# Storing rows and their factors from one tile, loading two experts' weights together, and joining statistics before the squares, in a two-layer attention and mixture-of-experts kernel

## The chip, the cores and the metric

The kernel runs on 1 core of one Trainium2 chip. The metric is the device time of one execution in microseconds (us), as the median of several runs; smaller is better.

## The reference

The input x has 8 batches of 256 tokens of 256 features (2048 tokens, fp32), and a context of the same size. Two layers follow, each an attention and a feed-forward part with residuals.

```python
x = x + _L0_xattn_ref(_layernorm(x), ctx, ctx, Wq, bq, Wout, bout)
x = x + _L0_ffn_ref(_layernorm(x), centroids, ln_g, ln_b, w1, b1, w2, b2)
x = x + _L1_xattn_ref(_layernorm(x), ctx, Wq, bq, Wkv, bkv, Wp, bp)
x = x + _L1_ffn_ref(_layernorm(x), gate_W, w1_e, w3_e, w2_e, w1_s, w3_s, w2_s)
```

- The attention of layer 0 is an autocorrelation: FFT products averaged over everything, the top 12 lags with softmax weights, a weighted sum of rolled values, and an output projection. Its result is added to x.
- The feed-forward of layer 0 assigns tokens to 8 experts in balance: expert e, in turn, takes the 256 tokens with the highest score (normalised row times its centroid) among those not yet taken. Each expert computes `routed + gelu(layer_norm(routed) @ w1 + b1) @ w2 + b2`, and the rows go back to their tokens.
- Layer 1 is a cross attention with 16 heads over the context, and a mixture of 8 experts (two for each token, 256 by 1024) beside 8 shared ones. It is the larger part of the time and the change does not touch it.

## The kernel before

**Staging.** Everything runs in one program. Its tokens lie as 16 tiles of 128 rows: `X` is [128, 16, 256], two tiles to a batch. Each engine runs its instructions in the order in which the program was written, and SP does the same with the DMAs that it issues; a DMA uses one of eight semaphores in turn, and waits for the DMA eight before it on the same one. So the order of the statements sets the order of the work, on each engine and in SP's queue. PE gets its spare work from a list of small steps (`work`): `fill` takes as many steps as should fill the time between two rounds of a search. Those are key and value projections of layer 1, and later the experts' products.

**The rows after attention, by batch (lines 1833 to 2003).** PE copies X's rows into PSUM by an identity matmul (`copy_rows`, 1833), adds the attention's row PB through a `spread` matrix (`spread_rows`, 1844), and the result goes back to X by an ACT copy. `column_norms` (1370, called at 1885) computes bounds for a later quantity: four small matmuls, an ACT scaling and two POOL operations. `small_products` (1866) are other small matmuls.

For the first three batches `take` (1990) computes raw `bn_stats` on DVE; for the fourth, ACT computes sums with the copy (`act_sums`, 2007) and then squares (2026); for the others DVE computes statistics whole (`tile_stats`). `put_together` (1971) turns six raw statistics into variances with six small POOL operations, `factors` (2039) calls `rstd` (1457), which starts with a POOL power (1465) and ends in `newton`, four small operations (1468 to 1471) for the reciprocal standard deviation. The factors (that and minus mean times it) lie in `rm`, [128, 16, 2]. `widen` (2043) spreads them to 32 columns, `factor_rows` (1950) turns them into rows of PSUM (`psr`), `factors_out` (2061) copies these to `srow`, and `times_factors` (2058) multiplies the raw scores with them. The two halves of expert 0's scores become `n`, those of all experts `SC`; SC's second half is made on POOL (2122).

**Through memory.** `SC` is stored to `SCd` (2173), from which `load_row` (2161) loads each expert's 2048 scores: a source of four outer steps (groups of 512 scores), each repeated to 32 partitions. The rows of X are stored to `NMd` in DRAM (2048 rows of 258), as each batch is done (2000 and 2017), and their factors into the last two columns by four stores of 8-byte pieces (`store_factors`, 1936). `Yd` (2177) is blanked, 2 MB, as is the end of `Od` (2181).

**The search (2184) and the list (2242).** For each expert, five rounds: DVE counts scores above a threshold (2198), PE sums the counts (`pcn`, 2215), DVE finds the next threshold. `list_tokens` makes the indices `ids` of the taken tokens with small matmuls, and POOL gathers their rows with factors from NMd into R (2323), in two gathers of 128 rows. Expert e's list is made while expert e+1 is searched. Then `ffn` (2358) is called: ACT normalises R (2367), PE transposes it (`turn_rows`, 2387), ACT writes RT (2391), PE multiplies with w1 (`ph`, 2404), and so on to the addition of b2b on DVE and the scatter to Yd (2431).

**Weights.** `load_l0` (1812) loads w1 and w2 of one expert, 1 MB each, into a pool of two buffers (w0). Those of expert 0 are loaded at 1822, those of expert 1 after the last `take`. Later ones follow as buffers come free.

The order around the change, as written:

```python
take(b[6:])
W0[1] = load_l0(1)
newton_3, means_3 = factors(12, 16, nc.vector)
newton_a(nc.vector)
widen(0, 8, nc.scalar)
...
nc.sync.dma_start(out=SCd, in_=SC)
for m in range(2):
    store_factors(m)
rows = {e: load_row(e) for e in range(1, 3)}
```

Of the kernel before, what the change touches and what calls it, by code (L numbers as in the profile page):

```python
# [9 lines left out]
F32 = mybir.dt.float32  # L10
# [9 lines left out]
P = 128  # L20
# [1066 lines left out]
def fast_path(  # L1087
# [33 lines left out]
    nc = tc.nc  # L1121
    B, S, D = x.shape
    T = B * S
    NT = T // P
    KC = D // P
    TPB = S // P
# [7 lines left out]
    NB = D // P  # L1134
# [12 lines left out]
    res = ctx.enter_context(tc.tile_pool(name="res", bufs=1))  # L1147
    small = ctx.enter_context(tc.tile_pool(name="small", bufs=3))
    dram = ctx.enter_context(tc.tile_pool(name="dram", bufs=1, space=DRAM))
    X = res.tile([P, NT, D], F32, name="X")  # L1150
    hn = ctx.enter_context(tc.tile_pool(name="hn", bufs=2))
    nfine = res.tile([P, 1], F32, name="nfine")
    bad0 = res.tile([P, 1], F32, name="bad0")
# [143 lines left out]
    for dst, src, i in (  # L1297
# [12 lines left out]
        out=WZ[:, :, DH : 2 * DH],  # L1310
# [59 lines left out]
    def column_norms(pn):  # L1370

        for c in range(NB):
            for kc in range(KC):
                nc.tensor.matmul(
                    pn[:, c : c + 1],
                    wsq[:, kc, c * P : (c + 1) * P],
                    ones[:, 0:1],
                    start=(kc == 0),
                    stop=(kc == KC - 1),
                )  # L1380
        nc.scalar.activation(qmax, pn, AF.Copy, scale=257.0)
        nc.gpsimd.tensor_tensor(
            qmax, qmax, powers[:, 1:2].to_broadcast([P, NB]), ALU.pow
        )
        nc.gpsimd.tensor_tensor(qmax, qmax, babs, ALU.add)
# [426 lines left out]
    def load_l0(e):  # L1812
        w1 = w0.tile([P, KC, F], F32, tag="w1", name=f"w1_{e}")
        nc.sync.dma_start(out=w1, in_=L0_ffn_w1[e].rearrange("(kc p) f -> p kc f", p=P))
        w2 = w0.tile([P, NF, D], F32, tag="w2", name=f"w2_{e}")
        nc.sync.dma_start(out=w2, in_=L0_ffn_w2[e].rearrange("(fc p) d -> p fc d", p=P))
        return w1, w2

    NMd = dram.tile([T, D + 2], F32, name="NMd")
    Yd = dram.tile([T, D], F32, name="Yd")  # L1820
    Td = dram.tile([E * CAP1 + P, ROW], F32, name="Td")
    Od = dram.tile([T + P, D], F32, name="Od")
    W0 = {0: load_l0(0)}


    order_b = [2 * g + m for m in range(2) for g in range(4)]
# [1 line left out]
    pos = {}  # L1828

    def rows_of(b):  # L1830
        return X[:, TPB * b : TPB * (b + 1), :]

    def copy_rows(b, pool, tag):
        pos[b] = pool.tile([P, TPB, D], F32, tag=tag, name="po")
        nc.tensor.matmul(
            pos[b].rearrange("p h d -> p (h d)"),
            ident,
            rows_of(b).rearrange("p h d -> p (h d)"),
            start=True,
            stop=False,  # L1840
            skip_group_check=True,
        )
# [23 lines left out]
    def small_products(j):  # L1866
        for dc in range(KC):
            nc.tensor.matmul(
                pw[:, j, :],
                wrt[:, dc, j * P : (j + 1) * P]  # L1870
                if j < 2
                else boc[:, dc : dc + 1].to_broadcast([P, P]),
                cenP[:, dc, :],
                start=(dc == 0),
                stop=(dc == KC - 1),
            )
# [2 lines left out]
    copy_rows(order_b[1], ps_t, "pt")  # L1879
    small_products(0)  # L1880
    small_products(1)
    copy_rows(order_b[2], ps_t, "pt")
    small_products(2)
    nc.tensor.matmul(pb, ones[:E, :], bdiag, start=True, stop=True)
    column_norms(pw[:, 4, 0:NB])
    nc.vector.tensor_copy(WCn, pw[:, 0:3, :])
    bound = pr.tile([P, E], F32, name="bound")
    nc.vector.tensor_copy(bound, pb)
# [44 lines left out]
    rowv = NMd.rearrange("(c p) d -> p c d", p=P)  # L1933
    sexp = pa.tile([P, NT, 32], F32, name="sexp")

    def store_factors(m):
        for h in range(TPB):
            nc.sync.dma_start(
                out=NMd.rearrange("(g m h p) d -> m h p g d", m=2, h=TPB, p=P)[m, h][
                    :, :, D:  # L1940
                ],
                in_=rm[:, 8 * m : 8 * m + 8, :].rearrange(
                    "p (g h) d -> h p g d", h=TPB
                )[h],
            )


    psrs = []
# [22 lines left out]
    def put_together(q1):  # L1971

        d, v = (
            small.tile([P, q1], F32, tag=f"pt_{x_}", name=f"pt_{x_}") for x_ in "dv"
        )
        m = MV[:, 0:q1, 0]
        nc.gpsimd.tensor_tensor(d, st6[:, :, 1], st6[:, :, 4], ALU.subtract)
        nc.gpsimd.tensor_tensor(v, st6[:, :, 2], st6[:, :, 5], ALU.add)
        nc.gpsimd.tensor_tensor(d, d, d, ALU.mult)
        nc.gpsimd.tensor_scalar(d, d, D / 4.0, None, ALU.mult)  # L1980
        nc.gpsimd.tensor_tensor(v, v, d, ALU.add)
        nc.gpsimd.tensor_scalar(MV[:, 0:q1, 1], v, 1.0 / D, None, ALU.mult)

        def means():
            nc.gpsimd.tensor_tensor(m, st6[:, :, 1], st6[:, :, 4], ALU.add)
            nc.gpsimd.tensor_scalar(m, m, 0.5, None, ALU.mult)

        return means

    def take(bs, raw=False):  # L1990

        for b in bs:
            for h in range(TPB):
                q = TPB * order_b.index(b) + h
                if raw:
                    nc.vector.bn_stats(st6[:, q, :], pos[b][:, h, :])
                else:
                    tile_stats(MV[:, q, :], pos[b][:, h, :])
            nc.scalar.copy(rows_of(b), pos[b])
            nc.sync.dma_start(  # L2000
                out=rowv[:, TPB * b : TPB * (b + 1), 0:D], in_=rows_of(b)
            )

    sums = pa.tile([P, NT, 2], F32, name="sums")
    sq = pa.tile([P, D], F32, name="sq")
# [1 line left out]
    def act_sums(b):  # L2007

        for h in range(TPB):
            q = TPB * order_b.index(b) + h  # L2010
            nc.scalar.activation(
                rows_of(b)[:, h, :],
                pos[b][:, h, :],
                AF.Identity,
                accum_out=sums[:, q, 0:1],
            )
        nc.sync.dma_start(out=rowv[:, TPB * b : TPB * (b + 1), 0:D], in_=rows_of(b))
        qs = slice(TPB * order_b.index(b), TPB * order_b.index(b) + TPB)
        nmean = small.tile([P, TPB], F32, tag="nmean", name="nmean")
        nc.gpsimd.tensor_scalar(nmean, sums[:, qs, 0], -1.0 / D, None, ALU.mult)  # L2020
        nc.gpsimd.tensor_scalar(MV[:, qs, 0], sums[:, qs, 0], 1.0 / D, None, ALU.mult)

        def squares():
            for h in range(TPB):
                q = TPB * order_b.index(b) + h
                nc.scalar.activation(
                    sq,
                    rows_of(b)[:, h, :],
                    AF.Square,
                    bias=nmean[:, h : h + 1],  # L2030
                    accum_out=sums[:, q, 1:2],
                )
            nc.gpsimd.tensor_scalar(
                MV[:, qs, 1], sums[:, qs, 1], 1.0 / D, None, ALU.mult
            )

        return squares

    def factors(q0, q1, eng):
        qs = slice(q0, q1)  # L2040
        return rstd(MV[:, qs, :], r2[:, qs], 1.0 + LN_EPS, LN_EPS**2, eng, mr2[:, qs])

    def widen(q0, q1, eng):
        dst = sexp[:, q0:q1, :]
        src = r2[:, q0:q1].unsqueeze(2).to_broadcast([P, q1 - q0, 32])
        if eng is nc.scalar:
            nc.scalar.copy(dst, src)
        else:
            eng.tensor_copy(dst, src)
# [16 lines left out]
    spread_rows(*b[4:6])  # L2066
    squares = act_sums(b[3])
    take(b[:3], True)
    squares()
    pcp = ps_t.tile([P, 32], F32, tag="pt", name="pcp")  # L2070
    for j in range(2):
# [5 lines left out]
    spread_rows(*b[6:])  # L2077
    cP = pa.tile([P, 32], F32, name="cP")
    nc.vector.tensor_tensor(cP, pcp, WCn[:, 2, :], ALU.add)
    raw_means = put_together(6)  # L2080
    newton_a, means_a = factors(0, 8, nc.gpsimd)

    def rows_part(ps, cols):

        for g in range(4):
# [12 lines left out]

    rows_part(ps0, cP[:, 0:1].to_broadcast([P, 32]))
    take(b[4:6])  # L2100
    newton_2, means_2 = factors(8, 12, nc.gpsimd)
    rows_part(psx, cP)
    take(b[6:])
    W0[1] = load_l0(1)
    newton_3, means_3 = factors(12, 16, nc.vector)
    newton_a(nc.vector)
    widen(0, 8, nc.scalar)
    factor_rows(0)
    factor_rows(1)
    factors_out(0)  # L2110
    newton_2(nc.vector)
    widen(8, 12, nc.vector)
    factor_rows(2)
    newton_3()
    widen(12, 16, nc.vector)
# [6 lines left out]
    nc.gpsimd.tensor_tensor(SC[:, halves[1]], sx1, srow[:, 1, :], ALU.mult)  # L2122
    raw_means()
    means_a()
    means_2(nc.gpsimd)
    means_3(nc.gpsimd)

# [31 lines left out]
    def load_row(e):  # L2161

        row = prow.tile([P, TB], F32, name=f"row{e}")
        sd = SCd[:, :]
        nc.sync.dma_start(
            out=row,
            in_=bass.AP(
                sd.tensor, sd.offset + e * TB, [[32 * TB, 4], [0, 32], [1, TB]]
            ),
        )  # L2170
        return row

    nc.sync.dma_start(out=SCd, in_=SC)
    for m in range(2):
        store_factors(m)
    rows = {e: load_row(e) for e in range(1, 3)}
    nc.sync.dma_start(
        out=Yd.rearrange("(c p) d -> p c d", p=P),
        in_=blank[:, 0:D].unsqueeze(1).to_broadcast([P, NT, D]),
# [177 lines left out]

    def ffn(e, ids, R):

        w1, w2 = W0.pop(e)  # L2360
        b2b = pf.tile([P, D], F32, tag="b2b", name="b2b")
        nc.sync.dma_start(out=b2b, in_=L0_ffn_b2[e].partition_broadcast(P))
        RT = pf.tile([P, KC, CAP], F32, tag="RT", name="RT")
        A = pf.tile([P, NF, CAP], F32, tag="A", name="A")
        Y = pf.tile([P, NCT, D], F32, tag="Y", name="Y")
# [1120 lines left out]
```

## Time and profile before

| quantity | value |
|---|---|
| median of three runs | 882.78 us (881.07 to 883.38) |
| the profiled execution's own time | 882.51 us |
| its span | 880.8 us, 1.7 us less |
| TensorE clock granted, mean | 0.993 |
| PE busy | 97% of the span |
| DVE, ACT, POOL busy | 310.0, 266.4, 214.2 us |
| DMA traffic | 105.22 MB, 119 GB/s on average |

The profile is of one execution. Busy times are sums over instructions; PE is TensorE's matmuls, PEld its weight loads beside them, DVE is VectorE, ACT ScalarE, POOL GpSimd and SP SyncE, which issues most DMAs. "SPq" in a timeline is the issue of a DMA, and "landing" the time from there to the last byte's signal. A line such as L2323 is a line of the kernel before. In a timeline the bracket at the end of a line is the engine's idle time ahead of the instruction, with what ended it. In a table of windows, each engine's busy time is followed by its number of instructions in brackets, and the last three columns are the TensorE clock (1.00 is full), the DMA engines' share and the traffic. Costs are read from the stretch where a wait ends last, not from the shares of the whole span.

### The profile page before, as it was taken

Reading aid. Unit: us, or ns where it says so; the run is one execution under the profiler, and the core shown is the slowest. Engines: PE = TensorE matmul, PEld = TensorE weight load, DVE = VectorE, ACT = ScalarE, POOL = GpSimd, SP = SyncE. Lnnn points to the kernel's source line nnn. Section 1 sums busy time; section 2 is a strip of 40 time slices with the busy share of each in tenths; the row PEclk is TensorE's granted clock in tenths of the full one; section 3 lists DMA queues with packets and bytes.
Section 4 is the critical chain, followed back from the end, with each engine's and each line's share of the span. In section 5 each row is a group of like instructions: output and inputs, shape, how many; then the busy total and the mean of one; then the engine's idle time right before and its main releaser. Section 6 shows DMA issues by size and latency. Waiting matters only on the chain. (4 is left out here: it accounts for less than half of the span.)

```text
span 880.8 us, 11150 instructions
## 1 busy us (share of the span) xinstructions
PE 858.4 (97%) x4180; PEld 535.4 (61%) x4180; DVE 310.0 (35%) x1022; ACT 266.4 (30%) x493; POOL 214.2 (24%) x298
## 2 busy tenths in 40 slices
PE   8988899999999999999999999999999999999997
PEld 6646687778555555545658474747464656474746
DVE  7376877321656665552111212011111111111011
ACT  4243453242577676331010111111111111111110
POOL 7251222211326464323310020111111122111200
PEclk9999999999999999999999999999999999999999
DMA  8474478850420001271210646565647443311130
GB/s 249 156 204 170 155 211 234 257 185 30 129 82 25 2 14 38 77 271 45 71 51 25 192 113 175 155 180 155 180 150 175 158 93 109 89 13 12 14 106 28
DMA packets 87127, 105.22 MB, mean 119 GB/s; under 512 B 8825, under 2 KB 77657, under 8 KB 87033
## 3 DMA queue, kind: packets, MB, share of 16 engines
q1 hardware_dynamic: 78520, 91.10, 32.7%
q0 software_dynamic: 7920, 13.02, 7.1%
q8 instruction: 35, 0.57, 0.3%
q10 hardware_dynamic: 624, 0.30, 0.1%
q14 instruction: 28, 0.22, 0.1%
HBM read 80.60 MB, written 25.37 MB: 120 GB/s over the span
## 5 line engine op out<-in xcount | busy, mean ns | idle before, releaser
L3115 DVE TENSOR_TENSOR A<-A,pu 128x512 f32<-128x512 f32 x96 | 66.0, 688 | 365.1 <-PE pu L3106 358.4
L3114 ACT ACTIVATE A<-pgt 128x512 f32<-128x512 f32 x96 | 57.4, 598 | 271.4 <-PE pgt L3106 271.4
L3175 POOL DMA_INDIRECT Od<-Y,ids x32 | 49.4, 1545 | 302.2 <-ACT Y L3188 207.7
L3106 PE MATMUL pgt<-RT,wa 128*128 128x512 f32 x256 | 121.1, 596 | 0.0
L3106 PE MATMUL pu<-RT,wb 128*128 128x512 f32 x256 | 120.3, 592 | 0.0
L3128 PE MATMUL py<-wc,A 128*128 128x256 f32 x512 | 111.8, 379 | 0.0
L3128 PEld LDWEIGHTS py<-wc,A 128*128 128x128 f32 x512 | 96.7, 190 | 13.3 <-issue 0.5
L3106 PEld LDWEIGHTS pu<-RT,wb 128*128 128x128 f32 x256 | 48.6, 190 | 61.2 <-issue 60.0
L2691 ACT ACTIVATE ex<-p,scale 128x512 f32<-128x512 f32 x128 | 77.3, 690 | 27.5 <-PE p L2683 26.2
L3106 PEld LDWEIGHTS pgt<-RT,wa 128*128 128x128 f32 x256 | 47.6, 190 | 54.9 <-issue 54.5
L2404 PE MATMUL ph<-RT,w 128*128 128x256 f32 x256 | 61.6, 389 | 1.5 <-ACT RT L2391 1.3
L2421 PE MATMUL py<-w,A 128*128 128x256 f32 x256 | 62.0, 389 | 0.0
L2404 PEld LDWEIGHTS ph<-RT,w 128*128 128x128 f32 x256 | 45.3, 190 | 9.9 <-ACT RT L2391 1.8
L2421 PEld LDWEIGHTS py<-w,A 128*128 128x128 f32 x256 | 46.5, 190 | 6.4
L2923 POOL DMA_INDIRECT Td<-HP,to x32 | 31.6, 988 | 65.7 <-DMA Td<-HP,to 62.7
L2413 ACT ACTIVATE A<-ph,b1c 128x256 f32<-128x256 f32 x64 | 30.1, 473 | 54.4 <-PE ph L2404 50.9
L3106 PE MATMUL pgt<-HT,wa_-1_2738 128*128 128x512 f32 x96 | 45.5, 596 | 0.0
L3106 PE MATMUL pu<-HT,wb_-1_2739 128*128 128x512 f32 x96 | 45.1, 592 | 0.0
L3188 ACT ACTIVATE Y<-py,R 128x256 f32<-128x256 f32 x32 | 15.2, 474 | 96.5 <-PE py L3128 96.5
L2683 PE MATMUL p<-QM,KT 32*128 32x512 f32 x256 | 43.4, 640 | 0.4 <-DVE QM L2664 0.4
L3128 PE MATMUL py<-wc_-1_2740,A 128*128 128x256 f32 x192 | 41.9, 379 | 0.0
L3128 PEld LDWEIGHTS py<-wc_-1_2740,A 128*128 128x128 f32 x192 | 36.4, 190 | 5.8 <-issue 1.0
(457 smaller groups left out, 990.6 us busy)
## 6 DMA issues: line engine op xcount, KB each, us to landing
w<-in_L_ffn_w_dram SPq DMA_DIRECT2D x16, 1024.0 KB, 6.9
wa<-in_L_ffn_w_e_dram SPq DMA_DIRECT2D x8, 1024.0 KB, 7.5
wb<-in_L_ffn_w_e_dram SPq DMA_DIRECT2D x8, 1024.0 KB, 8.8
wc<-in_L_ffn_w_e_dram SPq DMA_DIRECT2D x8, 1024.0 KB
R<-Td SPq DMA_DIRECT2D x8, 530.0 KB, 7.0
sa<-in_L_ffn_w_e_dram SPq DMA_DIRECT2D x16, 256.0 KB, 3.9
sb<-in_L_ffn_w_e_dram SPq DMA_DIRECT2D x16, 256.0 KB, 5.1
sc<-in_L_ffn_w_e_dram SPq DMA_DIRECT2D x16, 256.0 KB, 6.5
```

What stands on the lines that cost most here:

```text
L2404: nc.tensor.matmul(ph, w1[:, kc, f * P : (f + 1) * P], RT[:, kc, :], start=(kc == 0), stop=(kc == KC - 1),)
L2413: nc.scalar.activation(A[:, f, :], ph, AF.Gelu_apprx_tanh, bias=b1c[:, e, f : f + 1])
L2421: nc.tensor.matmul(py, A[:, f, r * P : (r + 1) * P], w2[:, f, :], start=(f == 0), stop=(f == NF - 1),)
L2683: nc.tensor.matmul(ps[g].rearrange("p m q -> p (m q)"), KT[rows, c, k0 : k0 + P], QM[b][rows, c].rearrange("p m q -> p (m q)"), start=True ...
L2691: nc.scalar.activation(e4[:, g], ps[g], AF.Exp, scale=scale)
L2923: nc.gpsimd.indirect_dma_start(out=Td, out_offset=bass.IndirectOffsetOnAxis(ap=to[g][:, k, j : j + 1], axis=0), in_=HP[:, GT * g + j, :], ...
L3106: nc.tensor.matmul(ps, w_[:, kc, fs], xs[kc], start=(kc == 0), stop=(kc == KC - 1),)
L3114: nc.scalar.activation(a, pgt, AF.Silu)
L3115: nc.vector.tensor_tensor(a, a, pu, ALU.mult)
L3128: nc.tensor.matmul(py, A[:, f, s : s + P], wc[:, f, :], start=(f == 0), stop=(f == NF - 1))
L3175: nc.gpsimd.indirect_dma_start(out=Od, out_offset=bass.IndirectOffsetOnAxis(ap=ids, axis=0), in_=Y, in_offset=None, compute_op=ALU.add,)
L3188: nc.scalar.activation(Y, py, AF.Copy, scale=R[:, i, D + e : D + e + 1])
```

## The change

- X becomes the first 256 columns of a tile `XF` with 258. POOL copies the factors into the last two columns (`keep_factors`, two copies), and four stores of four tiles each write rows and factors to NMd at once. They take the place of eight stores of rows, made as each batch was done, and of four stores of factors, and are issued after the loads of row1 and row2.
- The weights of expert 1 are loaded right behind those of expert 0. The bias row b2b is loaded with the weights, and lies in their pool.
- The six raw statistics are put together, and their power is started, ahead of ACT's squares on the program's list; the factors go in groups of 6, 6 and 4 columns in place of 8, 4 and 4. The first group's newton runs on POOL, both first widenings on ACT, one of them between the copies of the last two batches.
- `column_norms` moves up, between `small_products(1)` and the next copy of rows.

```diff
-    X = res.tile([P, NT, D], F32, name="X")
+
+    XF = res.tile([P, NT, D + 2], F32, name="X")
+    X = XF[:, :, 0:D]
...
-        return w1, w2
+        b2b = w0.tile([P, D], F32, tag="b2b", name=f"b2b_{e}")
+        nc.sync.dma_start(out=b2b, in_=L0_ffn_b2[e].partition_broadcast(P))
+        return w1, w2, b2b
...
-    W0 = {0: load_l0(0)}
+    W0 = {e: load_l0(e) for e in range(2)}
...
     small_products(1)
+    column_norms(pw[:, 4, 0:NB])
     copy_rows(order_b[2], ps_t, "pt")
     small_products(2)
     nc.tensor.matmul(pb, ones[:E, :], bdiag, start=True, stop=True)
-    column_norms(pw[:, 4, 0:NB])
...
-    def store_factors(m):
-        for h in range(TPB):
-            nc.sync.dma_start(
-                out=NMd.rearrange("(g m h p) d -> m h p g d", m=2, h=TPB, p=P)[m, h][
-                    :, :, D:
-                ],
-                in_=rm[:, 8 * m : 8 * m + 8, :].rearrange(
-                    "p (g h) d -> h p g d", h=TPB
-                )[h],
-            )
+    def keep_factors(m):
+        nc.gpsimd.tensor_copy(
+            XF[:, :, D:].rearrange("p (g m h) d -> p m g h d", m=2, h=TPB)[:, m],
+            rm[:, 8 * m : 8 * m + 8, :].rearrange("p (g h) d -> p g h d", h=TPB),
+        )
...
             nc.scalar.copy(rows_of(b), pos[b])
-            nc.sync.dma_start(
-                out=rowv[:, TPB * b : TPB * (b + 1), 0:D], in_=rows_of(b)
-            )
...
-        nc.sync.dma_start(out=rowv[:, TPB * b : TPB * (b + 1), 0:D], in_=rows_of(b))
...
     take(b[:3], True)
+    raw_means = put_together(6)
+    newton_a, means_a = factors(0, 6, nc.gpsimd)
     squares()
...
-    raw_means = put_together(6)
-    newton_a, means_a = factors(0, 8, nc.gpsimd)
-
...
     take(b[4:6])
-    newton_2, means_2 = factors(8, 12, nc.gpsimd)
+    newton_2, means_2 = factors(6, 12, nc.gpsimd)
+    newton_a()
     rows_part(psx, cP)
-    take(b[6:])
-    W0[1] = load_l0(1)
+    take(b[6:7])
+    widen(0, 6, nc.scalar)
+    take(b[7:])
     newton_3, means_3 = factors(12, 16, nc.vector)
-    newton_a(nc.vector)
-    widen(0, 8, nc.scalar)
+    newton_2(nc.vector)
+    widen(6, 12, nc.scalar)
     factor_rows(0)
     factor_rows(1)
     factors_out(0)
-    newton_2(nc.vector)
-    widen(8, 12, nc.vector)
     factor_rows(2)
     newton_3()
     widen(12, 16, nc.vector)
...
     raw_means()
     means_a()
-    means_2(nc.gpsimd)
+    means_2()
+    keep_factors(0)
     means_3(nc.gpsimd)
+    keep_factors(1)
...
     nc.sync.dma_start(out=SCd, in_=SC)
-    for m in range(2):
-        store_factors(m)
     rows = {e: load_row(e) for e in range(1, 3)}
+    for i in range(0, NT, 4):
+        nc.sync.dma_start(out=rowv[:, i : i + 4, :], in_=XF[:, i : i + 4, :])
...
-        w1, w2 = W0.pop(e)
-        b2b = pf.tile([P, D], F32, tag="b2b", name="b2b")
-        nc.sync.dma_start(out=b2b, in_=L0_ffn_b2[e].partition_broadcast(P))
+        w1, w2, b2b = W0.pop(e)
```

The operands of `copy_rows` lose their flattened form, since X's tiles now have gaps between them.

## Prediction

> **What bounds the kernel now.** I read the totals by engine first, then the table of 40 slices, then the table of windows of 2 us over the first 90 us, then the timeline of the two stretches in which that table shows PE short of work.
>
> ```profile
> span 880.8 us, 11150 instructions
> PE 858.4 (97%) x4180; PEld 535.4 (61%) x4180; DVE 310.0 (35%) x1022; ACT 266.4 (30%) x493; POOL 214.2 (24%) x298
> PE   8988899999999999999999999999999999999997
> ```
>
> PE is the bound: only 22.4 us (880.8 - 858.4) are open, and the slices put them before 250 us and in the last slice. The change removes no PE work of weight, so all it can win is idle time or half clock at the head. The chain of waits covers only the last 0.42 us and does not help.
>
> The windows (window, length, busy PE, PEld, DVE, ACT, POOL with counts, PE clock, DMA share, GB/s) show where the head loses:
>
> ```profile
> 72.00:74.00 2.00, 1.11 (x6) 0.63 (x4) 0.26 (x1) 0.60 (x2) 1.38 (x2) 1.00 1.05 364
> 74.00:76.00 2.00, 0.66 (x4) 0.61 (x5) 1.71 (x7) 0.00 (x0) 1.32 (x1) 1.00 1.03 325
> 76.00:78.00 2.00, 2.00 (x8) 1.41 (x7) 1.47 (x8) 0.74 (x2) 0.00 (x0) 0.55 0.59 209
> 78.00:80.00 2.00, 2.00 (x8) 1.52 (x7) 1.06 (x5) 0.38 (x1) 0.00 (x0) 0.59 0.27 98
> 80.00:82.00 2.00, 2.00 (x12) 1.50 (x11) 1.79 (x10) 0.75 (x2) 0.00 (x0) 1.00 0.27 97
> ```
>
> PE works 1.77 of the 4 us from 72 to 76, and then its clock is 0.55 to 0.59 for about 3.4 us. The timeline (start, duration, what, count, idle before and releaser) gives the reason:
>
> ```profile
> 58.72 0.34 SPq L2173 DMA_DIRECT2D SCd<-SC  x1
> 59.84 4.15 SPq L1938 DMA_DIRECT2D NMd<-rm  x4
> 67.46 1.27 SPq L2165 DMA_DIRECT2D row<-SCd  x2
> 68.78 0.47 SPq L2177 DMA_DIRECT2D Yd<-blank  x1
> 72.32 1.24 POOL L2323 DMA_INDIRECT R<-NMd,ids  x1 [5.84 <-PE pp L1412]
> 73.74 0.75 DVE L2190 SCALAR_TENSOR_TENSOR n<-n,lo,row 128x512 f32<-128x512 f32 x1 [2.33 <-DMA row<-SCd]
> 75.34 0.19 PE L2215 MATMUL pcn<-B32h,cnt 128*128 128x32 f16 x1 [2.23 <-DVE above L2198]
> 83.01 1.09 ACT L2367 ACTIVATE R<-R 128x256 f32<-128x256 f32 x2
> ```
>
> Search 1 waits 2.33 us for row1, PE 2.23 us behind it. Row1 is late because SCd landed 7.8 us after its issue, at about 66.5 us (the DMA view), behind W0[1]'s 2 MB issued at 54.08 and 54.97; a 256 KB transfer without that load ahead of it (Gd, 24 us) landed in 2.5 us.
>
> **The change part by part.**
>
> *W0[1] early.* W0[1] is issued with W0[0], at about 36 us. At the 350 to 370 GB/s of the windows the 4.25 MB of both are in by about 49 us, while the row stores, first at 46 us, are gone. SCd then has free queues: 2.5 us in place of 7.8. The two b2b loads are 128 KB each; those of later experts wait for a DVE addition of two experts before, done long ahead: nothing.
>
> *Statistics.* POOL now puts six columns together while ACT squares: pt_d starts when the last raw statistics are there (about 47.25 in place of 49.17). The power costs 1.67 us for 8 columns and 0.99 for 4; I take 1.32 for 6. So: powers at 49.1 to 50.4 and 51.05 to 52.4, newton_a (4 POOL operations of 0.20 to 0.25 with gaps) to 53.5, the last power to 54.5 in place of 55.02. It releases newton_3, psr(3), srow(1), n. One newton of 4 DVE operations and one widening go (5 times about 0.2 us). Gain 0.5 us; bounds 0.1 (newton_a on POOL costs 0.3 more than thought) and 0.9. It moves SCd's issue from 58.72 to about 58.25.
>
> *Column norms.* The PE work is the same and moves by about 1 us in a stretch where pr3 waits for CW (landing 38.55, PE's own backlog until 38.57). 0; small_products(2) now waits for ACT's reading of qmax, behind a row copy of 1.1 us on PE. If that cover goes, 0.3 us.
>
> *Rows and factors in one tile.* POOL does 10 small operations behind SC[1], two of them new copies of factors; 8 took 2.12 us, so 2.7. They stand behind SC[1], not ahead of it. SP loses eight row stores and four factor stores (4.15 us of SP time from 59.84), and gains four stores, each of 4 tiles by 258. SP's order becomes SCd, row1, row2, four NMd stores, Yd, Od, row3 on. Row1 waits only for SCd to land (58.25 + 2.5 = 60.75) and the POOL copies: issue 61.0 in place of 67.46. Its landing was 6.1 us after issue, behind nothing large (73.53); uncontended rows in the windows at 78 to 82 take 2.7 each. I take 65.5, bounds 63.7 and 67.1. Search 1's own list is ready (DVE idle starts) at 71.41, so even the latest bound hides it. **The 2.33 us stall goes**, PE keeps its fillers, and with PE busy the clock need not fall: the rounds' matmuls pcn stood at 75.34, 77.28, 79.85, 81.37, 82.90, so two steps of 1.94 and 2.57 against 1.53: 1.45 us. I take both: 0.5 + 2.33 + 1.45 = 4.28 us earlier at the end of search 1, about 78.7 in place of 83.0. If the half clock only moves elsewhere, 2.8.
>
> *What is late next.* The first gather R0 waits on POOL for all rows in NMd. Before, these were in by 67.3, 5 us ahead of the gather; now NMd is issued from about 62.3 behind two row loads.
>
> ```profile
> DMA packets 358, 0.39 MB, mean 97 GB/s; under 512 B 10, under 2 KB 346, under 8 KB 358
> q1 hardware_dynamic: 343, 0.35, 24.5%
> Yd<-blank SPq DMA_DIRECT2D x1, 2048.0 KB, 14.2
> ```
>
> The first two lines (the DMA view at 78 to 82) say that little but a quarter of the 16 engines works there, 24.5%, at 97 GB/s: four engines empty a queue that the others have long finished. The third (66 to 70) is that queue: 2 MB, 6.0 us at 350 GB/s, landed 14.2 us after issue behind two rows; most of its 16 parts landed at 75.97, the last four from 81.94 to 82.98. So the rows lie on four engines and what is queued behind them there waits. NMd is as large and takes the same place behind the same two loads. From the issue of row1 (67.46) to Yd's last part (82.98) were 15.5 us; from 61.0 that is 76.5, less up to 1 us for the gathers' packets, which shared those engines then and cannot now: **NMd by 76.0**. Bounds: 70.0 (no queueing: 62.3 + 1.75 + 6.0, where 1.75 is Gd's 2.5 less 0.75 for 256 KB at 350 GB/s) and 79.3 (below, under slower). I take 76.0, because Yd has the same size and place.
>
> Released 0.3 us on, the first gather is issued at 76.3, 4 us later than now (72.32), the second 1.54 behind (72.32 and 73.86 now), and it lands 4.4 us on, at 82.2 (6.1 in the crowd now, 3.3 for R1's pair alone). ACT wants that half from about 79.3 (78.7 and one of the two operations of 83.01). So **2.9 us are given back** as PE idle ahead of ph; one more or less for each us of NMd, 0 from 73.1 down. POOL has nothing else behind the gathers for 20 us; DVE goes on with search 2 until its matmul pcn stands behind the waiting transposes on PE.
>
> By the page DMA: Bandwidth & Descriptors of the Trainium skill, section Rules for kernel authors, one issues a DMA early and waits late; this change issues NMd late, which speaks against it. The trace agrees as far as the slack of 5 us goes that is used up. By the fit of the same page's section Anatomy of one DMA — SWDGE (gpsimd) path, made for DMAs that GpSimd issues (an estimate here: 2.0 us and bytes over 436 GB/s), NMd would be there 6.9 us after issue, at 69.2, the gather would not be late, and the sum would be 878.2.
>
> From 200 us on PE is the bound and carries a shift through; the stretch at 145 to 165 us, where the DMA share is above 1, is started by PE's work and shifts with it. Rows 3 to 6 are wanted from 96 us on and land from 84.
>
> **Sum.** -4.28 + 2.9 = -1.4 against the profiled execution of 882.51 (span 880.8 and 1.7 around it): **881.1**. That execution stands 0.27 below the median.
>
> **The rivals.** *The gather is not late* (NMd by 73 us): -4.28, **878.2**. For it: three quarters of NMd's parts lie on engines without rows, and the rows start without a crowd; against: a gather waits for the last part, and Yd's was late. *Nothing left over*: PE's new idle of 3 us ahead of ph is followed by half clock, as that of 72 to 76 was, and 1.45 us are lost again: -1.4 + 1.45, **882.6**; the same time follows if the clock falls once in any case or the early weights delay R3's loads and the row stores by that much. *Slower*: NMd's rows of 1032 bytes go at the pace of the row stores.
>
> ```profile
> q1 hardware_dynamic: 924, 0.88, 92.6%
> q1 hardware_dynamic: 197, 0.20, 27.3%
> ```
>
> The first is the DMA view at 49 to 53, row stores into the same rows of NMd: 0.926 x 16 x 4 us for 0.88 MB, 67 engine-us a MB; the second, 79.95 to 82, is Yd's end: 45. At 67 NMd's 2.1 MB take 8.8 us of each engine in place of 5.9, and NMd is in at 79.0 to 79.3. It decides from NMd at 77.4 on, where all 4.28 are spent; at 79.2 the loss is 6.1, and 6 us of PE idle bring the half clock's 1.45: -4.28 + 6.1 + 1.45 = +3.3, **885.8**. For it: those packets; against: at 47 to 49 the same stores ran at 49 engine-us a MB (0.68 MB, 103.6% of 2 us), so the wide figure may be their waiting for data.
>
> **How the numbers follow.** This kernel's measurement can tell 0.3%, 2.65 us: below 880.13, or above 885.43. Forecast 0.40, own range 879.6 to 882.3, of which 0.12 lies below 880.13; not late 0.24; nothing left over 0.18; slower 0.18, of which 0.04 lies below 885.43. Faster 0.36, same 0.28 + 0.18 + 0.04 = 0.50, slower 0.14. Range 877.8 to 885.4: it leaves out half of the last case and the lowest third of the second, 0.17.
>
> **What would show it.** Right: SCd lands within 3 us; no idle ahead of n in search 1; clock 1.00 from 71 us to the end of search 1; POOL's idle ahead of the first gather ends by DMA NMd, at about 76; ACT's first R<-R waits for R0, with PE idle of 3 us ahead of prt. Wrong: newton_3 later than 55.05; the first gather still at 72 (not late) or after 78 (slower); PE idle between 36 and 50 us that was not there; half clock after 80, which makes 882.6.

## The result, and the profile after

The changed kernel takes 884.3 us (median of 19 runs, 882.83 to 887.07), the kernel before 881.51 beside it (19 runs, 879.0 to 883.38). The ratio is 1.0034, with a 95% interval of 1.0024 to 1.0043: about 3.0 us slower, where 1.4 us faster was forecast. The time lies inside the range, on the other side of no change.

In the timelines, `n` is the list of scores that a search works on, `few` are the counts that DVE takes from PE's sums `pcn`, R0 are the gathered rows of expert 0 (`R`, two gathers of 128 rows), `prt` are PE's transposes of them and `ph` the products with w1. The page of the changed kernel's profile (totals and the first row of the slices) shows no more work, as it should:

```profile
span 881.6 us, 11135 instructions
PE 859.2 (97%) x4180; PEld 535.9 (61%) x4180; DVE 308.5 (35%) x1017; ACT 265.9 (30%) x494; POOL 214.0 (24%) x304
PE   8998899999999999999999999999999999999997
```

The profiled spans differ by 0.8 us only (881.6 against 880.8). The head tells what happened. SP's timeline, and below it lines of the timeline of DVE, POOL, ACT and PE from 70 us on:

```profile
56.87 0.34 SPq L2169 DMA_DIRECT2D SCd<-SC  x1
59.47 1.26 SPq L2161 DMA_DIRECT2D row<-SCd  x2
60.78 5.01 SPq L2172 DMA_DIRECT2D NMd<-X  x4
65.84 2.74 SPq L2173 DMA_DIRECT2D Yd<-blank  x1
```

```profile
70.22 0.75 DVE L2186 SCALAR_TENSOR_TENSOR n<-n,lo,row 128x512 f32<-128x512 f32 x1 [0.20 <-issue]
75.72 1.24 POOL L2319 DMA_INDIRECT R<-NMd,ids  x1 [10.57 <-PE pp L1414]
82.19 1.27 ACT L2361 ACTIVATE R<-R 128x256 f32<-128x256 f32 x2 [4.21 <-DMA R<-NMd,ids]
82.84 1.36 PE L2381 MATMUL prt<-ident,R 128*128 128x128 f32 x4 [3.31 <-ACT R L2361]
84.86 1.22 PE L2398 MATMUL ph<-RT,w 128*128 128x256 f32 x2 [0.66 <-ACT RT L2385]
86.14 0.19 DVE L2216 TENSOR_SCALAR_CACHE_REDUCE few<-pcn 128x32 f32<-128x32 f32 x1 [5.01 <-PE pcn L2211]
```

The row loads go 8 us earlier than before, and search 1 has no wait for row1 (0.20 us, by issue, where 2.33 were). The first gather went at 72.32 before; now it goes at 75.72, though the list it needs was made at about 70 and POOL stood idle. The releaser that its bracket names had long been done: what came last are the stores of NMd, whose last part landed at 74.64. So ACT waits 4.21 us for R0, PE 3.31 behind it, and search 2 on DVE 5.01, since its matmul stands behind the transposes on PE.

The windows of 2 us (columns as before: busy PE, PEld, DVE, ACT, POOL, PE clock, DMA share, GB/s):

```profile
74.00:76.00 2.00, 2.00 (x11) 1.50 (x10) 1.86 (x9) 0.73 (x2) 0.28 (x1) 1.00 0.90 299
78.00:80.00 2.00, 1.53 (x7) 1.02 (x7) 1.74 (x6) 0.00 (x0) 0.23 (x1) 1.00 0.53 174
80.00:82.00 2.00, 0.00 (x0) 0.00 (x0) 1.10 (x5) 0.00 (x0) 0.00 (x0) 1.00 0.26 101
82.00:84.00 2.00, 1.16 (x4) 0.58 (x4) 0.00 (x0) 1.73 (x4) 0.00 (x0) 0.59 0.27 102
84.00:86.00 2.00, 1.34 (x5) 0.78 (x4) 0.00 (x0) 1.02 (x2) 0.00 (x0) 0.50 0.29 111
86.00:88.00 2.00, 2.00 (x11) 1.46 (x9) 1.46 (x7) 0.82 (x2) 0.00 (x0) 0.50 0.26 102
88.00:90.00 2.00, 2.00 (x11) 1.65 (x8) 0.64 (x7) 0.61 (x2) 0.00 (x0) 0.71 0.26 101
```

The hole and the half clock of 72 to 80 are gone, as forecast. Both are there again six to eight us later, and larger: PE does nothing from 80 to 82, and the clock stands at half from 82.35 to 89.18 us, 6.8 us in place of 3.4. Over the whole head each of the two profiles has three windows of half clock of 3.41 us: from 38.67, 55.74 and 76.22 before, and from 55.04 and two from 82.35 after.

The same points in both traces say what it adds up to (us; counts are DVE's of PE's sums, five to a search):

| point | before | after | difference |
|---|---|---|---|
| first count of search 0 | 59.74 | 58.28 | -1.46 |
| last count of search 1 | 83.13 | 78.17 | -4.95 |
| first count of search 2 | 86.32 | 86.14 | -0.18 |
| last count of search 2 | 95.88 | 97.24 | +1.36 |
| first product's activation of layer 1's experts | 357.31 | 358.06 | +0.75 |

Five us are won up to the end of search 1, 4.8 lost in the wait and the slow transposes behind it, 1.5 more at half clock during search 2. The medians lie 2.8 us apart and the profiled executions 0.8; the profiled execution of before lies 1.0 above its median, and that of after 1.0 below, so the two profiles show the mechanism and not the whole size. The 19 executions of the changed kernel differ with their clock: those with a mean granted clock of 0.989 to 0.991 took 885.30 to 887.07 us, those with 0.994 or 0.995 took 882.83 to 884.36, and the profiled one had 0.994.

### The profile page after: what moved, and what is told of

Read it like the earlier page. It is cut to its first block, busy times and chain, and to the rows that moved or that the text cites. A ratio compares the mean times of both kernels' runs of the same rounds, so it can differ in the third digit from the quotient of the medians.

```text
span 881.6 us, 11135 instructions
## 1 busy us (share of the span) xinstructions
PE 859.2 (97%) x4180; PEld 535.9 (61%) x4180; DVE 308.5 (35%) x1017; ACT 265.9 (30%) x494; POOL 214.0 (24%) x304
## 4 chain that ended last, share of the span: by engine, by line
PE 89%; DVE 4%; POOL 3%; DMA 2%; ACT 1%; issue 1%; DVEq 0%; ACTq 0%; POOLq 0%
PE pgt L3100 19%; PE py L3122 19%; PE pu L3100 19%; PE py L2415 6%; PE ph L2398 5%; PE p L2677 4%; PE pv L2692 3%; DMA R<-NMd,ids 2%; PE pp L2743 2%; PE pp L2644 2%; PE pp L1393 2%; PE pp L1414 1%; PE pgu L3295 1%; PE pt L3156 1%; POOL x_r L1467 1%
## 5 line engine op out<-in xcount | busy, mean ns | idle before, releaser
L2398 PE MATMUL ph<-RT,w 128*128 128x256 f32 x256 | 63.7, 399 | 1.5 <-ACT RT L2385 1.3
```

Source lines behind the costliest of these rows:

```text
L2398: nc.tensor.matmul(ph, w1[:, kc, f * P : (f + 1) * P], RT[:, kc, :], start=(kc == 0), stop=(kc == KC - 1),)
```

## The experiments

All ratios are to the kernel before, run beside each kernel on the same chip, with 95% intervals. The theory: the stores of rows and factors, now behind two row loads, make R0 late; PE's idle time brings half clock; both together undo the gain. The rivals: the early weights or the other parts cost, or the half clock fell where it did by chance.

**The stores ahead of the row loads.** In the changed kernel:

```diff
-    rows = {e: load_row(e) for e in range(1, 3)}
     for i in range(0, NT, 4):
         nc.sync.dma_start(out=rowv[:, i : i + 4, :], in_=XF[:, i : i + 4, :])
+    rows = {e: load_row(e) for e in range(1, 3)}
```

> The changed kernel with one thing altered: the four stores of rows and factors stand ahead of the loads of row1 and row2 on SP. Theory (late gather: the stores wait behind two row loads on four engines, R0 lands at 82 to 83, PE idles 4 us and then runs two windows of 3.4 us at half clock, which undoes the 5 us won up to the end of search 1): rows are in by 67, the first gather is issued at about 70, R0 is there before search 1 ends, no idle ahead of prt, no half clock after 80; row1 lands just about when search 1 wants it (70). The time falls about 6 us under the changed kernel, to about 877 to 879, ratio to before 0.995 to 0.997. Rival (the loss comes from the early weights or from where the half-clock windows happen to fall, not from the gather): about 884, ratio 1.003, with R0 early.

0.9955 (0.9938 to 0.9971). One statement moved past another turns 3 us of loss into 4 of gain. Lines of its timeline:

```profile
70.41 1.24 POOL L2319 DMA_INDIRECT R<-NMd,ids  x1 [5.69 <-DMA row<-SCd]
70.68 0.75 DVE L2186 SCALAR_TENSOR_TENSOR n<-n,lo,row 128x512 f32<-128x512 f32 x1 [2.34 <-DMA row<-SCd]
79.83 0.60 PE L2381 MATMUL prt<-ident,R 128*128 128x128 f32 x4
```

Search 1 waits 2.34 us for row1 again, now behind the stores, the gather goes 5 us earlier, and the transposes have no idle time ahead of them (no bracket) and take 0.60 us, not 1.36. So the loss comes with the stores' place behind the row loads. PE idled 2.24 us ahead of 72.28 there, and the clock stayed at 1.00 until 101, so an idle time of that size need not bring half clock.

**Row loads on 16 engines.** The scores stand four times in SC's rows, so that the source of a row load has 16 outer steps:

```diff
-        nc.vector.tensor_copy(cenP[:, kc, 0:E], pc)
+        nc.vector.tensor_copy(
+            cenP[:, kc, :].rearrange("p (j e) -> p j e", e=E),
+            pc.unsqueeze(1).to_broadcast([P, 4, E]),
+        )
...
-                sd.tensor, sd.offset + e * TB, [[32 * TB, 4], [0, 32], [1, TB]]
+                sd.tensor, sd.offset + e * TB, [[8 * TB, 16], [0, 8], [1, TB]]
```

> The changed kernel with one thing altered: the scores of the 8 experts stand four times in SC's rows, so that a row load has a source of 16 outer steps in place of 4; order of SP as changed. Theory (a row load keeps four engines busy for 2.7 us and what is queued behind it there is late): a row load now takes about 1 us on all engines, NMd is in by 69 to 70, the gather goes at about 70, no idle ahead of prt: 877 to 879, ratio 0.995 to 0.997, as with the stores first. Rival (stores late for another reason, such as their 1032-byte rows or their issue on SP): NMd still in at 73 or later, R0 late, 882 to 884.

0.9999 (0.9982 to 1.0017): a miss. The stores landed at 71.46, 11.7 us after the first one's issue (59.77), in place of 13.9 in the changed kernel (60.78 to 74.64), so the four engines of the row loads were 2.2 us of it and not all. (Of the 16 parts of the changed kernel's last store, twelve were in by 68.90 and the other four from 73.97 to 74.64; here all 16 came in from 69.17 to 71.46.) Search 1 ended 7.0 us earlier than before, and the idle time was there again:

```profile
72.53 1.24 POOL L2322 DMA_INDIRECT R<-NMd,ids  x1 [8.14 <-PE pp L1414]
79.99 0.69 PE L2384 MATMUL prt<-ident,R 128*128 128x128 f32 x2 [2.48 <-ACT R L2364]
```

with half clock from 79.77 to 86.60.

**The parts alone.** In the kernel before, the weights early (`W0 = {e: load_l0(e) for e in range(2)}`):

> The kernel before with one part of the change alone: expert 1's weights loaded behind expert 0's. Theory: SCd lands within 3 us, row1 is there before search 1 wants it, and the row stores stay early, so R0 is not late either: 2.3 us of wait and one half-clock window (1.5 to 1.7 us) less, few of search 1 at -3.5 us, 877 to 879, ratio 0.996 to 0.997. Rival (the early weights are what costs): 882 to 885.

0.9956 (0.9938 to 0.9973): the early weights are worth 4 us. Row1 goes at 64.74 in place of 67.46, search 1 has no wait of 1 us or more for it, and its last count is at -3.18.

The statistics (`put_together` and the first `factors` ahead of `squares()`, groups of 6, 6, 4, first newton on POOL):

> The kernel before with one part of the change alone: the joined statistics ahead of the squares, factors in groups of 6, 6, 4, newton on POOL. Theory: search 0 starts about 1.4 us earlier, but SCd still lands behind expert 1's weights, so search 1 still waits for row1 and nothing is left of it at search 1's end: within 1 us of before, ratio 0.999 to 1.001. Rival (the statistics carry their gain through): -1.4 us, ratio 0.998.

0.9999 (0.9986 to 1.0011). Search 0 starts 2.5 us earlier, search 1 waits 3.97 us for row1, and its last count is at -0.81: earlier work that meets the same late transfer. (The kernel before has half-clock windows at 38.67 and 55.74 that this profile has not, so not all of the 2.5 us is the statistics'.)

The stores (`XF`, `keep_factors`, four stores behind row2):

> The kernel before with one part of the change alone: rows and factors in one tile, stored by four stores behind the loads of row1 and row2; weights late, statistics and norms as before. Theory: SCd still lands at 66.5, rows are issued there, NMd lands 13 to 14 us after row1's issue, at 80 to 81, the gather follows and R0 is there at 86 to 88 where ACT wants it at 83; PE idles 3 to 5 us and has two half-clock windows: 4 to 8 us slower, ratio 1.005 to 1.009. Rival (the later stores alone cost nothing that can be measured): ratio 0.999 to 1.001.

1.0028 (1.0013 to 1.0042): slower, by 2.5 us where 4 to 8 were expected, and not by that way. SCd landed in time and row1 was issued at 60.84: without the row stores ahead of them in SP's queue, the weights of expert 1 went at 37.95 in this kernel, with no change to where they are written. So the stores' part brings the weights' gain with it, and still loses. Half clock follows here too, for one window (85.86 to 89.27):

```profile
60.84 1.26 SPq L2159 DMA_DIRECT2D row<-SCd  x2
62.15 5.63 SPq L2170 DMA_DIRECT2D NMd<-X  x4
77.53 1.24 POOL L2317 DMA_INDIRECT R<-NMd,ids  x1 [10.73 <-DMA Od<-blank]
84.34 0.44 PE L2381 MATMUL prt<-ident,R 128*128 128x128 f32 x2 [3.54 <-ACT R L2361]
```

**Weights and statistics, and all but the stores.**

> The kernel before with two parts of the change: expert 1's weights early, and the joined statistics ahead of the squares. Rows and factors are stored as before, column norms stand where they stood. Theory (these two parts gain, the later stores take it back): the gains add, search 1 ends about 5.5 us earlier than before (3.2 from the weights alone and 2.4 from search 0's earlier start), the first gather follows its list without a wait at about 70, no idle ahead of prt: 4 to 5.7 us under before, ratio 0.9935 to 0.9955. Rival (an earlier search 1 only meets the half clock or a late R0 there, whatever the stores): ratio 0.998 to 1.002.

0.9946 (0.9927 to 0.9966), last count of search 1 at -6.39, and R0 in time: in its timeline ACT and PE meet no wait for it.

```profile
69.47 1.24 POOL L2323 DMA_INDIRECT R<-NMd,ids  x1 [5.07 <-PE pp L1412]
76.62 1.09 ACT L2367 ACTIVATE R<-R 128x256 f32<-128x256 f32 x2
77.93 0.60 PE L2387 MATMUL prt<-ident,R 128*128 128x128 f32 x4
```

> The whole change without its stores: early weights with b2b in their pool, joined statistics, moved column norms; rows are stored as each batch is done and factors by four small stores, as before. Theory: as the weights with the statistics, 0.9946; R0 is in time, no idle ahead of prt: ratio 0.992 to 0.996. Rival (b2b's move or the moved norms cost what is missing): 0.998 or more.

0.9946 (0.993 to 0.9961): the whole change without its stores is 4.8 us faster than the kernel before. b2b's move and the norms cost nothing that shows.

**Column norms back** in the changed kernel:

> The changed kernel with one part undone: column norms back behind the third small product. Theory: they cost and bring nothing; R0 is as late as in the changed kernel, idle ahead of prt 2 to 4 us: ratio to before 1.000 to 1.005. Rival (the moved norms delay or speed the head): first count of search 0 moves by over 0.5 us, and the ratio by over 0.001 from the changed kernel's 1.0034.

1.0037 (1.0021 to 1.0053), as the change itself.

**Work put into the wait.** In the changed kernel, ahead of expert 0's transposes:

```diff
             prt = ps_t.tile([P, KC, NCT, P], F32, tag="pt", name="prt")
+            if e == 0:
+                for _ in range(5):
+                    nc.tensor.matmul(
+                        prt.rearrange("p k r q -> p (k r q)"),
+                        w1[:, 0, 0:P],
+                        w1[:, 0, 0 : KC * NCT * P],
+                        start=True,
+                        stop=True,
+                    )
```

> The changed kernel with work added and nothing taken away: five matmuls of 128 by 512, whose sums are overwritten, stand ahead of expert 0's transposes on PE, in the idle time of 3.3 us in which PE waits for R0. Theory (the wait itself costs 4 us, and the half clock that follows idle PE another 3): with PE kept busy the clock stays at 1.00 after 82, R0 is as late as it was; about 2.5 to 3.5 us under the changed kernel run beside it, ratio to before 0.999 to 1.001, in spite of 3 us more PE work. Rival (the half clock there has nothing to do with the idle): as slow as the changed kernel or slower, 1.003 to 1.006, with half clock after 82.

> The changed kernel once more, unaltered, beside the others. Theory: R0 lands at 82 to 84, PE idles 3 us or more ahead of prt, two windows of 3.4 us at half clock follow: ratio 1.002 to 1.005. Rival (the profile shown of it was one chance placement of the half clock): no half clock after 82 here, and a ratio under 1.001.

With the added work 0.9997 (0.9983 to 1.0011); the changed kernel unaltered, beside it, 1.0017 (1.0002 to 1.0031). The windows, first of the changed kernel again, then with the work:

```profile
80.00:82.00 2.00, 0.04 (x1) 0.04 (x1) 0.00 (x0) 0.60 (x1) 0.00 (x0) 0.51 0.26 103
84.00:86.00 2.00, 1.46 (x4) 1.09 (x5) 0.17 (x2) 0.94 (x2) 0.00 (x0) 0.50 0.30 111
88.00:90.00 2.00, 2.00 (x6) 1.46 (x6) 0.41 (x7) 0.47 (x1) 0.00 (x0) 0.50 0.21 80
```

```profile
80.00:82.00 2.00, 2.00 (x6) 0.94 (x5) 1.29 (x5) 0.00 (x0) 0.00 (x0) 1.00 0.27 105
84.00:86.00 2.00, 1.34 (x10) 0.94 (x8) 0.14 (x2) 1.02 (x2) 0.00 (x0) 1.00 0.26 102
88.00:90.00 2.00, 2.00 (x12) 1.62 (x11) 1.83 (x11) 1.44 (x3) 0.00 (x0) 1.00 0.26 102
```

R0 is as late in both (the gather at 75.24 and 75.86). PE does 4.45 us of useless work, its clock stays at 1.00 where it stood at half for 10.2 us, and the kernel is no slower for it, by the middles of the intervals 1.8 us faster (the intervals overlap by a little). The same holds over all twelve executions of each: the mean granted clock is 0.9959 with the work and 0.9919 without, which is 7 us less at half clock. Search 2 takes 9.55 us from its first count to its last (85.86 to 95.41), as in the kernel before (9.56), and 11.79 without the work (85.83 to 97.62). So the idle time, and not chance, brings the half clock here. The repeat came out at 1.0017, a little under what was expected, with all that was expected in its profile.

**Other orders.** Stores first and row loads on 16 steps:

> The changed kernel with the stores of rows and factors ahead of the row loads, and the row loads on a source of 16 outer steps. Theory: stores first cost search 1 a wait for row1 of 2.3 us (seen with the stores first alone); with a row load of under 1 us on all engines that wait shrinks to under 1 us, R0 is still there in time: 1 to 2 us under the kernel with the stores first, ratio 0.9925 to 0.9945. Rival (row1 waits for the stores' bytes on any engine): the wait stays at 2 us or more, ratio 0.995 to 0.997.

0.9942 (0.992 to 0.9964), with no wait of 1 us or more for row1 or ahead of prt. Row1, the stores, row2:

> The changed kernel with the order row1, four stores of rows and factors, row2 on SP, and row loads on a source of 16 outer steps. Theory: row1 lands by 64 and search 1 doesn't wait for it; the stores land 1 us later than with the stores first, by 70 to 71, so the gather goes at 71 to 72 and R0 lands at 78 to 79, about when ACT wants it: 0.5 to 2 us under the kernel with the stores first, ratio 0.9925 to 0.995. Rival (the stores' own pace of 8 us or more is too slow behind any row load): R0 lands at 80 or later, PE idles over 1 us, ratio 0.997 to 1.001.

0.9995 (0.9976 to 1.0014): the time that the rival gives. The stores were in at 70.8 and the gather went at 71.79, but its second half landed at 80.41, 7.1 us after its issue in the crowd with Yd, and search 1 had ended at 76.6. PE idled 1.62 and 1.09 us and had half clock from 81.3 to 88.1.

**The pitch of NMd's rows.** The stores still took 9.4 us with nothing ahead of them (60.31 to 69.68, stores first, 16 steps), and 10.6 with the row loads behind them on four engines (58.83 to 69.47). One cause that could be tried is that rows lie 1032 bytes apart in memory; three kernels have them 1088 apart (258 of 272 columns stored, the rest blanked early):

```diff
-    NMd = dram.tile([T, D + 2], F32, name="NMd")
+    NMd = dram.tile([T, D + 16], F32, name="NMd")
```

> The changed kernel with the rows of NMd 1088 bytes apart in memory in place of 1032 (258 of 272 columns stored, the rest blanked early by one more store, the gather takes whole rows). Theory (row loads hold four engines, and rows at 1032 bytes store slowly): the stores' packets stay near 47 ns; the last part still waits behind row1 and row2 on four engines, so NMd is in about 13 to 14 us after row1's issue in place of 15, R0 1 to 2 us earlier, 1 to 2 us under the changed kernel: ratio 0.999 to 1.003. Rival (the pitch has no part in it): packets and landings as in the changed kernel, 1.002 to 1.005.

> The kernel with the order row1, stores, row2 and row loads on 16 steps, with rows 1088 bytes apart. Theory (pitch): the stores take 6 to 7 us of transfer in place of 10, are in by 68 in place of 71, the gather goes with its list at about 70, R0 is there by 76 to 77, no idle ahead of prt: ratio 0.992 to 0.995, against 0.9995 without the pitch. Rival (not the pitch): stores in at 71, 0.998 to 1.001.

> The kernel with the stores ahead of the row loads on 16 steps, with rows 1088 bytes apart. Theory (pitch): the stores end about 3 us earlier, row1 lands well before search 1 wants it, the idle for it goes: 0.991 to 0.994, against 0.9942. Rival (not the pitch): as without it, 0.993 to 0.996, stores in 10 us after their issue.

1.0031 (1.0018 to 1.0044), 0.999 (0.9971 to 1.0008) and 0.9946 (0.9924 to 0.9967), with the stores in at 74.60, 69.99 and 68.53. From the first store's issue that is 14.6, 10.9 and 10.0 us, where it was 13.9, 11.3 and 9.4 with the old pitch. So 1088 gives no gain beyond the spread of 9.4 to 10.6; other pitches were not tried.

## Why the prediction was wrong

*Weights early: right.* SCd landed in 2.0 us (56.87 to 58.89) for a forecast of 2.5, and row1 at 65.85 for 65.5. Alone the part is worth 4 us.

*Statistics: right, a little small.* Where both kernels of a pair had their half-clock windows at the same places, search 0 starts 0.61 us earlier (59.11 with the stores first on 16 steps, 59.72 with the weights alone) and 0.98 (58.28 after, 59.26 with the stores alone), for a forecast of 0.5. The larger differences of other pairs hold a half-clock window at 38.7 or 55 that one of the two has not.

*Column norms: right,* nothing.

*The stall for row1 and its half clock: right, with some luck.* 4.95 us earlier at the end of search 1, 4.28 forecast. Search 0 starts 1.46 us earlier; by the pairs above 0.61 to 0.98 of it is the statistics', and the other 0.48 to 0.85 goes with the window at 38.67 that only the profile of before has. Without that, 4.1 to 4.5 is left.

*The late gather: right, with errors that cancel.* NMd by 76.0 was forecast and 74.64 measured, R0's second half at 82.2 and 82.83, the idle time ahead of the expert's work 2.9 and 3.31. Between the two, the gather was put 0.3 us behind NMd and went 1.08 behind it (0.95 to 1.17 in the other kernels where it waited for the stores), and its second half was given 4.4 us to land and took 5.6. The reading of Yd, 14.2 us behind two row loads, carried this. Its explanation by four engines was only part: with the row loads on 16 engines the stores still take 11.7 us, 2.2 less.

*The clock: this step failed.* The sum "-4.28 + 2.9 = -1.4" leaves the clock at full speed after the new idle time. The half clock behind it was a rival of its own ("nothing left over"), priced at "1.45 us are lost again", one window of 3.4 us, with a chance of 0.18. It belonged in the sum, and at two windows. What it cost in the profile: the transposes 1.36 in place of 0.60, the first pair of ph 1.22 in place of 0.70, and 11.10 us from the first to the last count of search 2 in place of 9.56: 0.76 + 0.52 + 1.54 = 2.8 us. With -4.28 + 2.9 + 2.8 the sum is +1.4, on the right side. The lines of the kernel before, then of the changed kernel with the added work, in which R0 is as late and the clock at 1.00:

```profile
84.32 0.60 PE L2387 MATMUL prt<-ident,R 128*128 128x128 f32 x4
85.57 0.70 PE L2404 MATMUL ph<-RT,w 128*128 128x256 f32 x2 [0.65 <-ACT RT L2391]
```

```profile
79.56 4.45 PE L2381 MATMUL prt<-w 128*128 128x512 f32 x10
83.85 0.60 PE L2390 MATMUL prt<-ident,R 128*128 128x128 f32 x4
85.10 0.70 PE L2407 MATMUL ph<-RT,w 128*128 128x256 f32 x2 [0.66 <-ACT RT L2394]
```

The rival "slower" gave 885.8, 3.3 us above the kernel before, which is near the 3.0 measured; its condition, NMd in at 79.0 to 79.3, did not come about, so that nearness says nothing for it.

What brings half clock can be read from the traces. Up to 190 us every half clock lasted 3.41, 6.83 or 10.24 us, so each trace's own clock changes set a grid of windows of 3.41 us, and PE's busy time can be read window by window. In the window ahead of the half clock at 82.35, PE was busy 0.59 us; with row1 first, where two idle times of 1.62 and 1.09 us stood close together, 0.69 us. With the stores first, the 2.24 us of idle time lay across two windows with 2.51 and 2.08 us busy, and the clock stayed up. From 10 to 190 us in the 17 profiles, half clock followed each of the 28 windows at full clock in which PE was busy 1.76 us or less, and three of those with 1.77 to 2.13. Above that it followed only three, all from about 35 us, ahead of the half clock near 38.6, which this does not explain. Once at half, the clock came back after windows with 3.06 us busy or more, and not after those with 0.77 to 2.76. Behind the late R0 the transposes and first products wait for ACT, so it took two windows in the changed kernel, three in its repeat and one with the stores alone.

The Trainium skill, page TensorE: Matmul & The Clock Gate, section "What's actually happening", has TensorE at half clock after an idle window of about 3.4 us, on a grid that runs freely, and back after one that was busy. This case's trace agrees in the length (3.41 us, 6.83 and 10.24 are one, two and three of them). It differs in what is enough: here PE need not be idle for a whole window, about half of one will do.

What stays open: the profiled executions differ by 0.8 us and the medians by 2.8. Windows at half clock also stood near 39, 55, 103 and 167 us in some profiles and not in others of kernels with the same order there, each worth up to 1.7 us; the grid starts at another moment in each execution and falls differently on the same idle times. Whether they make up the rest was not shown. Nor was it settled why the stores take 9.4 us with nothing ahead: in the stores-first kernel with 16 steps the traffic falls from 317 GB/s (61 to 65 us) to 265 (65 to 69) with the engines as busy (94.0% and 104.7%).

## What to carry to other kernels

Moving a store behind loads, in one queue, moves its readers too: price the last landing against the moment when the reader wants it after everything else became faster, and not against where the reader stands now. Here a transfer that was 3.3 us late for TensorE cost those 3.3 us and 2.8 more at half clock; a wait of that size belongs in the sum with its clock, and how many windows it brings depends on where it falls and on how busy TensorE is behind it. Five matmuls of useless work put into the wait, 4.45 us of PE time, kept the clock up and cost no time (0.9997 of before with them, 1.0017 without). And when statements go from a queue, look at what stood behind them: here removing the row stores moved the weights by 16 us (54.08 to 37.95) without a line of theirs being touched.

## What the runs showed that was not expected

- TensorE need not idle through a window of 3.41 us to fall to half clock: being busy for 1.76 us of one or less was enough every time.
- The same four stores take 13.9 us from their issue behind two row loads on four engines, 11.7 behind two on sixteen, and 9.4 to 10.6 ahead of both; 6 would follow from the pace of Yd's end (45 engine-us a MB).
- A gather lands 5.9 us after issue in the crowd of the stores-first kernel, 7.1 where row1 is first and the stores and Yd are a little later, and 2.9 to 3.7 for the second pair of the kernel before, outside such a crowd: a gather's own landing grows with what is queued ahead of it, and search 1, which ended 2 us earlier there (76.58 and 78.64), wanted it sooner.
